# A selective scan on one core: the forcing term built from token-major blocks scaled by B and transposed, in place of products with diagonals of B

## The chip, the core and the metric

The kernel runs on one core of a Trainium2 chip. Its time is the time on the device, in microseconds, from one launch to the end; several runs are taken, and their median is the figure. Of one execution there is also a profile: for each engine (TensorE for matrix products, VectorE, ScalarE, GpSimd, SyncE for DMA), what it ran and what it waited for. The kernel before takes 28995.0 us, the median of three runs from 28984.81 to 29002.8.

## What is computed

The input `x` is an image of 256 x 256 positions with 128 channels. Two layers are applied, each to a group-normalised `x` and each added to `x`. Layer 0 is attention within rows, with a gate. Layer 1, where the change lies, is a two-dimensional selective scan. Cut to what matters:

```python
# layer 1; d = 256 channels, N = 16 states, L = 256 * 256 positions, K = 4 directions
xin, z = split(x @ in_proj_w.T)                  # 256 channels each
xc  = silu(conv3x3_depthwise(xin) + conv_b)
xs  = [xc by rows, xc by columns, rows reversed, columns reversed]
dts, B, C = split(xs @ x_proj_w)                 # 8, 16 and 16 numbers a position, for each k
dt  = softplus(dts @ dt_proj_w + dt_proj_b)
for l in range(L):                               # for each k, channel, state n
    h = h * exp(dt[l] * A[n]) + (dt[l] * xs[l]) * B[l, n]
    y[l] += h * C[l, n]                          # summed over n
y = sum over the four directions of (y + Ds * xs), brought back to one order
out = (layernorm(y) * silu(z)) @ out_proj_w.T
```

So for each direction, each of 256 channels and each of 16 states a recurrence runs over 65536 positions. Its forcing term is `(dt * x) * B[n]`: a factor of channel and position by a factor of state and position.

## The kernel before

**Tiling.** Layer 0 takes about the first 3.3 ms. Layer 1 then passes over the image four times, for the directions k = 0, 2, 1, 3 in this order. A pass has 64 chunks of 4 rows or columns, T = 1024 positions ("tokens"). Channels lie on the 128 partitions, in two blocks (j = 0, 1), and tokens along the free axis. A chunk has 32 units, each one channel block j and one state n: eight units (m = 0 to 7) for each of (g, j) = (0, 0), (0, 1), (1, 1), (1, 0), with n = 8g + m. There are 256 x 32 = 8192 units. Unit numbers below are places in a chunk, 0 to 31.

**A unit** needs a decay `exp(dt * A)` (`decay`, L854, ScalarE), a feed (the forcing term), a scan over 1024 tokens on VectorE (`scan`, L936), the scan's last column copied as the next chunk's start (`carry`, L950, ScalarE), a product of the states by C (`times_c`, L944) and a sum over n of the products (`add_up`, L910: eight 128 x 128 transposes on TensorE, which accumulate in PSUM into a tile with tokens on the partitions). Four kinds of unit share the work out (`KINDS`, by m: "AACBACCB" for k = 0, "AABBAABE" for the others; E is a B where (g, j) = (1, 1)):

- A: the decay goes to PSUM; GpSimd makes the feed, `xu * b`, with B of this state broadcast to all partitions by a DMA (`feed`, L861, `load_b`); GpSimd makes the product by C.
- C: as A, but VectorE makes the product by C.
- B: the decay goes to SBUF; TensorE makes the feed, in PSUM (`feed_turned`, L874); VectorE makes the product by C.
- E: TensorE makes the feed, GpSimd the product by C.

So 16 of the 32 units in a chunk of the last three passes have a feed by TensorE (m = 2, 3, 6, 7 in each of four groups), and 8 of 32 in the first pass (m = 3, 7).

**TensorE's feed** works from a transposed copy of `u = dt * x`, `dtuT`, with tokens on the partitions: [token, block of 128 tokens t, channel]. For each t, a matrix product has the 128 tokens x 128 channels of `dtuT` on one side and, on the other, a diagonal matrix that holds B[:, n] of these 128 tokens: it transposes the block back to [channel, token] and multiplies by B at once. `diagonal` (L867) makes such a diagonal on ScalarE, as the identity times one column of B per token. Eight diagonals make a set for one state n; both channel blocks use it, and there are seven sets (`dgs`). TensorE runs an fp32 product as two hardware instructions, so the eight products of a unit are 16 in the profile.

**Rings.** Two PSUM slots "s" hold a decay (A, C) or a feed (B, E); four SBUF buffers "w" hold the feeds, decays or states; four "hc" hold products by C; three "b" and eight "c" the broadcast rows.

**Order.** The order is written out by hand (`manual_schedule`): each engine runs its instructions in the order in which the program issues them. `step(u)` (L1015) is called for each unit u and issues, in this order, the copy of the last scan's end, the decay of u + 1 (or of B and E units up to three ahead), GpSimd's feed of u + 3, transposes of finished products, TensorE's feed of u + 1, side work, diagonals, then the scan of u and its product by C.

Diagonals come from a queue: `plan` (L956) enters eight for each state with a first and a due unit, and `run_diagonals` (L1007) issues up to `RATE` of them a step, none in a step in which a ScalarE piece of side work was issued, unless due. The first unit allowed is that in which the set seven sets older is used last.

Side work (`prep`, `finish`, `adds`, `normalise`) is cut into pieces by generators, and `run_sides` (L981) issues up to `PIECES` TensorE pieces in a step, by u % 4. `prep` of the chunk after next or the next computes the convolution (first pass), the projections to B, C and dt (L581 to L605), the softplus of dt on ScalarE, `u = dt * x` on GpSimd (`xu`, L616), and the transposes of B and of u (`dtp` in its names) to `bT` and `dtuT`. `adds` adds the residual term by products with a diagonal of D (`dD`, L793) and the sums of earlier passes, in PSUM, to y. The transposes of u wait for unit 22 of the chunk before, or later:

```python
yield from through(at1 + 3 + j if k == 0 else max(22, at1 + 4 + j), [
```

Of the kernel before, what the change touches and what calls it, by code (L numbers as in the profile page):

```python
# [15 lines left out]
P = 128  # L16
# [297 lines left out]
def _layer1(tc, ctx, const, dram, ident, vec, mr, a, x1, x1T, out):  # L314
# [88 lines left out]
    hcs = Ring(p1, "hc", 4, [P, T])  # L403
    brs = Ring(p1, "b", 3, [P, T])
    crs = Ring(p1, "c", GS, [P, T])
    dgs = Ring(p1, "dg", 7, [P, TB, P])
    dtuTs = Ring(p1, "dtuT", 2, [P, TB, D])
    bTs = Ring(p1, "bT", 2, [P, TB, ST])

# [59 lines left out]
    def prep(i):  # L469
# [165 lines left out]
        yield from through(0, [(f"btp_{i}", [turn_b], leave_b)])  # L635
        w["dtuT"] = dtuTs.take(f"dtuT_{i}")
        for j in range(ND):
            yield from through(at1 + 3 + j if k == 0 else max(22, at1 + 4 + j), [
                turned(
                    w["dtuT"][:, 4 * q : 4 * q + 4, j * P : (j + 1) * P],  # L640
                    lambda u, q=q: xu[j][:, (4 * q + u) * P : (4 * q + u + 1) * P],
                    f"dtp_{i}_{j}_{q}",
                )
                for q in range(QT)
            ], "e")
            w["ready"] = j + 1
# [185 lines left out]
        kind = KINDS[work[u // SU][0]][u % GS]  # L832
        return ("B" if kind == "E" and u % SU // GS == 2 else kind) in kinds

    in_psum, in_sbuf, states, prod, bt, ct, diag = {}, {}, {}, {}, {}, {}, {}
    fed = [u for u in range(total) if is_kind(u, "AC")]

    def load_b(r):
# [21 lines left out]
        in_sbuf[u] = ops.take(f"w_{u}")  # L860
        nc.gpsimd.tensor_tensor(in_sbuf[u], live[i]["xu"][j], bt.pop(u), ALU.mult)  # L861

    def diagonal(i, n, t):

        if t == 0:
            diag[i, n] = dgs.take(f"dg_{i}_{n}")
        nc.scalar.mul(diag[i, n][:, t, :], ident, live[i]["bT"][:, t, n : n + 1])  # L867

    def feed_turned(u):
        i, p, g, j, n, m = at(u)  # L870
        assert live[i]["ready"] > j and not any(t[2:4] == (i, n) for t in queue)
        in_psum[u] = slots.take(f"s_{u}")
        for t in range(TB):
            nc.tensor.matmul(  # L874
                in_psum[u][:, t * P : (t + 1) * P], live[i]["dtuT"][:, t, j * P : (j + 1) * P],
                diag[i, n][:, t, :], start=True, stop=True,
            )

    def load_sum(i, j):

# [70 lines left out]


    queue = []
    uses = []

    def plan(i):  # L956


        for g in range(2):
            for m in range(GS):  # L960
                u = SU * i + 2 * GS * g + m
                if is_kind(u, "BE"):
                    uses.append(u + GS)
                    s = uses[-1 - dgs.n] - 1 if len(uses) > dgs.n else -SU
                    for t in range(TB):
                        queue.append((s, u - 2, i, g * GS + m, t))

    RATE = {0: (1, 2, 2, 1), 1: (2, 3, 3, 2), 2: (2, 3, 3, 2), 3: (2, 3, 3, 2)}
    PIECES = {0: (2, 2, 2, 3), 1: (1, 1, 1, 2), 2: (1, 1, 1, 2), 3: (1, 1, 1, 2)}
    sides = []  # L970

    class Side:
# [31 lines left out]
                sides.remove(d)  # L1004
        return taken

    def run_diagonals(u, most):  # L1007
        while queue and queue[0][0] <= u and (most > 0 or queue[0][1] <= u):
            if live[queue[0][2]].get("bT") is None:
                assert queue[0][1] > u  # L1010
                return
            diagonal(*queue.pop(0)[2:])
            most -= 1

    def step(u):  # L1015
# [38 lines left out]
        if q == 3 and is_kind(u + 3, "BE"):  # L1054
            decay(u + 3)
        if ok(u):
            run_diagonals(u, 0 if taken else RATE[work[i][0]][q])
            scan(u)
            times_c(u)
        while after:  # L1060
# [23 lines left out]
    with tc.manual_schedule():  # L1084
        whole(prep(0))
        plan(0)
        for r in range(brs.n):
            load_b(r)
        for m in range(GS):
            load_c(0, m)  # L1090
        sides.append(Side(prep(1), 0))
        for u in range(-14, -4):
            run_sides(u)
        run_diagonals(0, 2 * TB)
        for u in range(-4, total + 2 * SU):
            step(u)
            if u >= total + 4 and not sides:
                break
        assert not (sides or queue or late or after or prod or states)
# [83 lines left out]
```

## Time and profile before

The profiled execution has a span of 28988.8 us. Its rows, for the whole span:

| what | busy us | share | instructions |
|---|---|---|---|
| VectorE | 26363.1 | 91% | 17323 |
| TensorE products | 25085.4 | 87% | 169780 |
| GpSimd | 24175.9 | 83% | 10253 |
| ScalarE | 20821.1 | 72% | 41137 |
| TensorE weight loads | 19655.6 | 68% | 169780 |
| span of the profiled execution | 28988.8 | | |
| median of three runs | 28995.0 | | |

The mean clock granted to TensorE is 0.945 of full speed. The rows that the change touches, as groups of instructions, with the mean of one: feeds on TensorE 57344 of 291 ns, transposes of products 65536 of 280 ns, diagonals on ScalarE 14336 of 392 ns, GpSimd's products by C 4416 of 2363 ns and its feeds 4608 of 2364 ns, scans on VectorE 2335 to 2347 ns.

How to read this: a busy time on TensorE is not work at its peak, since its products are pipelined and their ends modelled. In a group's row, the last part is idle time of the engine just before these instructions and the instruction that ended most of it. A wait for several instructions is put down to the one that came last.

### The profile page before, as it was taken

Reading aid. Unit: us, or ns where it says so; the run is one execution under the profiler, and the core shown is the slowest. Engines: PE = TensorE matmul, PEld = TensorE weight load, DVE = VectorE, ACT = ScalarE, POOL = GpSimd, SP = SyncE. Lnnn points to the kernel's source line nnn. Section 1 sums busy time; section 2 is a strip of 40 time slices with the busy share of each in tenths; the row PEclk is TensorE's granted clock in tenths of the full one; section 3 lists DMA queues with packets and bytes.
Section 4 is the critical chain, followed back from the end, with each engine's and each line's share of the span. In section 5 each row is a group of like instructions: output and inputs, shape, how many; then the busy total and the mean of one; then the engine's idle time right before and its main releaser. Section 6 shows DMA issues by size and latency. Waiting matters only on the chain. (4 is left out here: it accounts for less than half of the span.)

```text
span 28988.8 us, 455370 instructions
## 1 busy us (share of the span) xinstructions
PE 25085.4 (87%) x169780; PEld 19655.6 (68%) x169780; DVE 26363.1 (91%) x17323; ACT 20821.1 (72%) x41137; POOL 24175.9 (83%) x10253
## 2 busy tenths in 40 slices
PE   8888888899988888888888888888888888888888
PEld 5555566666666677777777677777777667667666
DVE  7888799999999999999999999999999888888888
ACT  4555566666666777777777777777777777777777
POOL 3444588888888899999999999999999888888888
PEclk8888899999999999999999999999999999999999
DMA  3111366666666666666666666666666555555555
GB/s 97 56 55 55 120 232 231 232 233 233 233 233 232 235 232 234 233 230 235 231 236 233 222 228 225 223 226 224 224 228 204 187 186 190 183 187 188 183 189 170
DMA packets 2487616, 5803.35 MB, mean 200 GB/s; under 512 B 189921, under 2 KB 1248152, under 8 KB 2485400
## 3 DMA queue, kind: packets, MB, share of 16 engines
q1 hardware_dynamic: 2475896, 5739.62, 58.8%
q0 software_dynamic: 9504, 34.61, 0.4%
q8 instruction: 1339, 21.94, 0.3%
q14 instruction: 877, 7.18, 0.1%
HBM read 5236.61 MB, written 536.87 MB: 199 GB/s over the span
## 5 line engine op out<-in xcount | busy, mean ns | idle before, releaser
L944 POOL TENSOR_TENSOR hc<-w,c 128x1024 f32<-128x1024 f32 x4416 | 10413.3, 2363 | 2079.1 <-DVE w L936 1320.7
L861 POOL TENSOR_TENSOR w<-xu,b 128x1024 f32<-128x1024 f32 x4608 | 10863.0, 2364 | 442.1 <-DMA b<-bc 78.7
L910 PE MATMUL y<-ident,hc 128*128 128x128 f32 x65536 | 8668.4, 280 | 1520.6 <-POOL hc L944 867.7
L910 PEld LDWEIGHTS y<-ident,hc 128*128 128x128 f32 x65536 | 7528.2, 144 | 3126.6 <-issue 1135.0
L936 DVE TENSOR_TENSOR_SCAN w<-s,hst,w 128x1024 f32<-128x1024 f32 x3840 | 8868.8, 2335 | 585.2 <-ACT s L854 331.4
L874 PE MATMUL s<-dg,dtuT 128*128 128x128 f32 x57344 | 7674.3, 291 | 1860.1 <-DVE w L936 1250.8
L874 PEld LDWEIGHTS s<-dg,dtuT 128*128 128x128 f32 x57344 | 7174.9, 203 | 2982.7 <-DVE w L936 1099.1
L936 DVE TENSOR_TENSOR_SCAN s<-w,hst,s 128x1024 f32<-128x1024 f32 x3008 | 7059.2, 2347 | 1263.2 <-PE s L874 1218.8
L854 ACT ACTIVATE s<-dt,negA 128x1024 f32<-128x1024 f32 x4608 | 5149.6, 1118 | 107.7 <-ACT hst L950 0.2
L867 ACT ACTIVATE dg<-ident,bT 128x128 f32<-128x128 f32 x14336 | 4827.9, 392 | 6.6 <-PE s L874 0.4
L944 DVE TENSOR_TENSOR hc<-s,c 128x1024 f32<-128x1024 f32 x3776 | 4622.9, 1224 | 203.1 <-DMA c<-bc 4.0
L854 ACT ACTIVATE w<-dt,negA 128x1024 f32<-128x1024 f32 x3584 | 4095.0, 1143 | 155.8 <-POOL hc L944 155.2
L950 ACT COPY hst<-s 128x1 f32<-128x1 f32 x3776 | 586.6, 155 | 4293.0 <-DVE hc L944 4097.1
L186 POOL TENSOR_TENSOR bias<-tri,mk 128x2048 f32<-128x2048 f32 x256 | 1164.0, 4547 | 1462.3 <-DVE ss L204 1303.7
L525 PE MATMUL cv<-xn,wtap 128*128 128x512 f32 x4608 | 2134.5, 595 | 10.3 <-ACT xn L514 10.3
L936 DVE TENSOR_TENSOR_SCAN s<-s,hst,w 128x1024 f32<-128x1024 f32 x768 | 1795.4, 2338 | 0.5 <-ACT s L854 0.4
L950 ACT COPY hst<-w 128x1 f32<-128x1 f32 x4416 | 808.4, 183 | 844.6 <-DVE w L936 805.7
L210 ACT ACTIVATE ss<-ss,nm 128x256 f32<-128x256 f32 x2048 | 866.5, 497 | 740.4 <-DVE nm L208 739.5
L936 DVE TENSOR_TENSOR_SCAN w<-w,hst,s 128x1024 f32<-128x1024 f32 x576 | 1346.0, 2337 | 2.6 <-PE s L874 2.1
L525 PEld LDWEIGHTS cv<-xn,wtap 128*128 128x128 f32 x4608 | 805.5, 190 | 702.6 <-issue 687.9
L616 POOL TENSOR_TENSOR xu<-dt,xu 128x1024 f32<-128x1024 f32 x512 | 1199.8, 2360 | 78.5 <-DMA b<-bc 78.5
L602 PE MATMUL dp<-xd,dtw 8*128 8x512 f32 x2048 | 1116.3, 640 | 0.3 <-ACT dt L605 0.3
(171 smaller groups left out, 22400.8 us busy)
## 6 DMA issues: line engine op xcount, KB each, us to landing
b<-bc SPq DMA_DIRECT2D x4608, 512.0 KB, 4.1
c<-bc SPq DMA_DIRECT2D x4096, 512.0 KB, 6.7
xc_d<-xu SPq DMA_DIRECT2D x256, 512.0 KB, 5.2
yrow_d<-ys SPq DMA_DIRECT2D x128, 1024.0 KB
xu<-xc_d SPq DMA_DIRECT2D x256, 512.0 KB, 6.2
yl<-yrow_d SPq DMA_DIRECT2D x512, 256.0 KB, 6.9
xcT_d<-xs SPq DMA_DIRECT2D x128, 512.0 KB, 2.9
xl<-xc_d SPq DMA_DIRECT2D x128, 512.0 KB, 7.1
```

The costliest lines, as they stand in the source:

```text
L186: nc.gpsimd.tensor_tensor(bias, tri.rearrange("p b h k -> p (b h) k"), st["mk"][:, r : r + 1, :].to_broadcast([P, NB * H, N]), ALU.add,)
L525: nc.tensor.matmul(pc, wtap[:, j, t, :], xn[:, 2 * q + u : 2 * q + u + 2, v : v + N], start=t == 0, stop=t == 8,)
L602: [lambda pt, j=j, q=q: nc.tensor.matmul(pt, dtw[:, k, j, :], xd[0:R, q * 512 : (q + 1) * 512], start=True, stop=True)],
L616: nc.gpsimd.tensor_tensor(xu[j], dt[j], xu[j], ALU.mult)
L854: nc.scalar.activation(dA, live[i]["dt"][j], AF.Exp, scale=negA[:, work[i][0] * ND + j, n : n + 1])
L861: nc.gpsimd.tensor_tensor(in_sbuf[u], live[i]["xu"][j], bt.pop(u), ALU.mult)
L867: nc.scalar.mul(diag[i, n][:, t, :], ident, live[i]["bT"][:, t, n : n + 1])
L874: nc.tensor.matmul(in_psum[u][:, t * P : (t + 1) * P], live[i]["dtuT"][:, t, j * P : (j + 1) * P], diag[i, n][:, t, :], start=True, stop=True,
L910: nc.tensor.matmul(w["y"][:, t, :], hc[:, t * P : (t + 1) * P], ident, is_transpose=True, start=first and t % 4 == 0, stop=last and t % 4 ...
L936: nc.vector.tensor_tensor_scan(rev(states[u]), rev(a), rev(b), hst[k][:, j, n : n + 1], ALU.mult, ALU.add)
L944: eng.tensor_tensor(prod[u], states[u], ct[i, n], ALU.mult)
L950: nc.scalar.copy(hst[k][:, j, n : n + 1], states.pop(u)[:, end : end + 1])
```

## The change

The feed of B and E units still works from `dtuT` and ends in PSUM with channels on the partitions, but its two steps are divided differently. For each state n and block t, `scale_b` multiplies the 128 tokens x 256 channels of `dtuT` by B[:, n], one number per partition (token), and writes both channel blocks, each to its slot of `bxs`. ScalarE does this for seven of the eight blocks t, GpSimd for t = 3. TensorE then transposes the scaled blocks of 128 x 128 by the identity, eight for a unit, with one hardware instruction each.

`bxs` has seven slots of [128, 8, 128], as many bytes as the seven sets of diagonals; a state takes two slots, one for each channel block, and each is free again after its feed. The queue's first unit becomes u - 14, its due unit stays u - 2, and a scaling waits until both channel blocks of `dtuT` are there (`ready`) and two slots are free. The transposes of u to `dtuT` may now be issued from `at1 + 4` for both blocks, rather than from unit 22. `PIECES` gives side work two TensorE pieces in every step of the last three passes (one in three steps of four and two in the fourth before), and three in the first two of each four steps of the first pass (two before).

```diff
--- before.py
+++ after.py
@@ -403,7 +403,9 @@
     hcs = Ring(p1, "hc", 4, [P, T])
     brs = Ring(p1, "b", 3, [P, T])
     crs = Ring(p1, "c", GS, [P, T])
-    dgs = Ring(p1, "dg", 7, [P, TB, P])
+    NBX = 7
+    bxs = p1.tile([P, NBX, TB, P], F32, tag="bx", name="bxs")
+    bx_free = list(range(NBX))
     dtuTs = Ring(p1, "dtuT", 2, [P, TB, D])
     bTs = Ring(p1, "bT", 2, [P, TB, ST])
 
@@ -635,7 +637,7 @@
         yield from through(0, [(f"btp_{i}", [turn_b], leave_b)])
         w["dtuT"] = dtuTs.take(f"dtuT_{i}")
         for j in range(ND):
-            yield from through(at1 + 3 + j if k == 0 else max(22, at1 + 4 + j), [
+            yield from through(at1 + 3 + j if k == 0 else at1 + 4, [
                 turned(
                     w["dtuT"][:, 4 * q : 4 * q + 4, j * P : (j + 1) * P],
                     lambda u, q=q: xu[j][:, (4 * q + u) * P : (4 * q + u + 1) * P],
@@ -832,7 +834,7 @@
         kind = KINDS[work[u // SU][0]][u % GS]
         return ("B" if kind == "E" and u % SU // GS == 2 else kind) in kinds
 
-    in_psum, in_sbuf, states, prod, bt, ct, diag = {}, {}, {}, {}, {}, {}, {}
+    in_psum, in_sbuf, states, prod, bt, ct, scaled = {}, {}, {}, {}, {}, {}, {}
     fed = [u for u in range(total) if is_kind(u, "AC")]
 
     def load_b(r):
@@ -860,21 +862,27 @@
         in_sbuf[u] = ops.take(f"w_{u}")
         nc.gpsimd.tensor_tensor(in_sbuf[u], live[i]["xu"][j], bt.pop(u), ALU.mult)
 
-    def diagonal(i, n, t):
+    def scale_b(i, n, t):
 
         if t == 0:
-            diag[i, n] = dgs.take(f"dg_{i}_{n}")
-        nc.scalar.mul(diag[i, n][:, t, :], ident, live[i]["bT"][:, t, n : n + 1])
+            scaled[i, n, 0], scaled[i, n, 1] = sorted((bx_free.pop(0), bx_free.pop(0)))
+        s0, s1 = scaled[i, n, 0], scaled[i, n, 1]
+        dst = bxs[:, s0 : s1 + 1 : s1 - s0, t, :]
+        src = live[i]["dtuT"][:, t, :].rearrange("p (j d) -> p j d", j=ND)
+        b = live[i]["bT"][:, t, n : n + 1]
+        if t == 3:
+            nc.gpsimd.tensor_scalar(dst, src, b, 1.0, ALU.mult, ALU.mult)
+        else:
+            nc.scalar.mul(dst, src, b)
 
     def feed_turned(u):
         i, p, g, j, n, m = at(u)
-        assert live[i]["ready"] > j and not any(t[2:4] == (i, n) for t in queue)
+        assert not any(t[2:4] == (i, n) for t in queue)
         in_psum[u] = slots.take(f"s_{u}")
+        slot = scaled.pop((i, n, j))
         for t in range(TB):
-            nc.tensor.matmul(
-                in_psum[u][:, t * P : (t + 1) * P], live[i]["dtuT"][:, t, j * P : (j + 1) * P],
-                diag[i, n][:, t, :], start=True, stop=True,
-            )
+            nc.tensor.transpose(in_psum[u][:, t * P : (t + 1) * P], bxs[:, slot, t, :], ident)
+        bx_free.append(slot)
 
     def load_sum(i, j):
 
@@ -951,7 +959,6 @@
 
 
     queue = []
-    uses = []
 
     def plan(i):
 
@@ -960,13 +967,11 @@
             for m in range(GS):
                 u = SU * i + 2 * GS * g + m
                 if is_kind(u, "BE"):
-                    uses.append(u + GS)
-                    s = uses[-1 - dgs.n] - 1 if len(uses) > dgs.n else -SU
                     for t in range(TB):
-                        queue.append((s, u - 2, i, g * GS + m, t))
+                        queue.append((u - 14, u - 2, i, g * GS + m, t))
 
     RATE = {0: (1, 2, 2, 1), 1: (2, 3, 3, 2), 2: (2, 3, 3, 2), 3: (2, 3, 3, 2)}
-    PIECES = {0: (2, 2, 2, 3), 1: (1, 1, 1, 2), 2: (1, 1, 1, 2), 3: (1, 1, 1, 2)}
+    PIECES = {0: (3, 3, 2, 3), 1: (2, 2, 2, 2), 2: (2, 2, 2, 2), 3: (2, 2, 2, 2)}
     sides = []
 
     class Side:
@@ -1004,12 +1009,13 @@
                 sides.remove(d)
         return taken
 
-    def run_diagonals(u, most):
+    def run_scales(u, most):
         while queue and queue[0][0] <= u and (most > 0 or queue[0][1] <= u):
-            if live[queue[0][2]].get("bT") is None:
-                assert queue[0][1] > u
+            s, due, i, n, t = queue[0]
+            if live[i].get("bT") is None or live[i]["ready"] < ND or (t == 0 and len(bx_free) < 2):
+                assert due > u, (u, due, live[i]["ready"], bx_free)
                 return
-            diagonal(*queue.pop(0)[2:])
+            scale_b(*queue.pop(0)[2:])
             most -= 1
 
     def step(u):
@@ -1054,7 +1060,7 @@
         if q == 3 and is_kind(u + 3, "BE"):
             decay(u + 3)
         if ok(u):
-            run_diagonals(u, 0 if taken else RATE[work[i][0]][q])
+            run_scales(u, 0 if taken else RATE[work[i][0]][q])
             scan(u)
             times_c(u)
         while after:
@@ -1091,7 +1097,7 @@
         sides.append(Side(prep(1), 0))
         for u in range(-14, -4):
             run_sides(u)
-        run_diagonals(0, 2 * TB)
+        run_scales(0, 2 * TB)
         for u in range(-4, total + 2 * SU):
             step(u)
             if u >= total + 4 and not sides:
```

## The prediction

> **What bounds the kernel now.** I read the page's rows of busy time first, then the windows view with one window for each of the four passes of layer 1 (directions 0, 2, 1, 3; their borders are the first and last scans in the timeline), because the page's averages mix layer 0 with four passes whose limits differ.
>
> ```profile
> core 0: us, PE busy (x) PEld busy (x) DVE busy (x) ACT busy (x) POOL busy (x), PEclk, DMA share, GB/s
> 3342.00:9903.00 6561.00, 5857.97 (x31900) 4159.94 (x31899) 6212.63 (x3328) 4442.65 (x7864) 5717.02 (x2494) 0.93 0.68 232
> 9903.00:16014.00 6111.00, 5354.79 (x39162) 4448.75 (x39161) 5681.48 (x2881) 4638.23 (x9595) 5551.53 (x2367) 0.98 0.69 233
> 16014.00:22054.00 6040.00, 5178.77 (x37115) 4279.13 (x37113) 5679.93 (x2882) 4667.29 (x9616) 5548.99 (x2369) 0.97 0.66 225
> 22054.00:28947.00 6893.00, 5835.07 (x40089) 4815.70 (x40088) 6047.28 (x4077) 5366.21 (x10622) 5961.24 (x2617) 0.93 0.56 187
> ```
>
> Divided by 64 chunks: the second pass takes 95.5 us a chunk, of which VectorE works 88.8 and GpSimd 86.7; the third 94.4, 88.7, 86.7; the first 102.5, 97.1, 89.3; the fourth 107.7, 94.5, 93.1, with ScalarE at 83.8. So VectorE is the bound, GpSimd 2 us behind it in the middle passes, and all that any change of feeding can win is VectorE's idle time, 5.4 to 13.2 us a chunk. What ends that idle time, by pass (waits view of VectorE, second pass, then fourth):
>
> ```profile
> DVE s L936 <- PE s L874: 333.7, 206, 4.6
> DVE w L936 <- POOL w L861: 34.5, 50, 0.7
> ...
> DVE s L936 <- PE s L874: 385.9, 227, 3.3
> DVE w L936 <- ACT s L854: 314.7, 265, 2.2
> ```
>
> The scans wait for TensorE's feeding products (L874): 5.2 us a chunk in the second pass. In the fourth ScalarE's decays (L854) cost another 4.9. The timeline shows how such a wait of 2.02 us arises, at unit 14 of a chunk (places 0 to 31 below):
>
> ```profile
> 13469.51 2.36 POOL L944 TENSOR_TENSOR hc<-w,c 128x1024 f32<-128x1024 f32 x1
> ...
> 13471.92 1.09 PE L910 MATMUL y<-ident,hc 128*128 128x128 f32 x8 [0.41 <-POOL hc L944]
> ...
> 13476.93 1.95 PE L874 MATMUL s<-dg,dtuT 128*128 128x128 f32 x16
> ...
> 13478.92 2.35 DVE L936 TENSOR_TENSOR_SCAN s<-w,hst,s 128x1024 f32<-128x1024 f32 x1 [2.02 <-PE s L874]
> ```
>
> The GpSimd row is unit 9's product by C, ending at 13471.87; TensorE stands in order behind it, then has 5.0 us of other work before the feed and 1.95 in it. GpSimd has worked without a pause since unit 4, so the feed is late because GpSimd is.
>
> **What the Trainium skill says.** "TensorE: Matmul & The Clock Gate", Part 4: a transpose is a product in transpose mode, which doesn't count as TensorE activity for its clock in the same way. The trace agrees on the form, not clearly on the clock: an fp32 product of L874 takes two instructions (57344 for 28672), a transpose of L910 one. "ScalarE: Activation LUTs", What ACT_TABLE_LOAD costs: 0.833 ns an element. "GPSIMD Engine Reference", 4.1 Engine selection: one-input work is near line rate, two-input work isn't; 3.1: 512 elements took 769 ns in a good one-input loop.
>
> **The change, part by part.** The prices:
>
> ```profile
> L944 POOL TENSOR_TENSOR hc<-w,c 128x1024 f32<-128x1024 f32 x4416 | 10413.3, 2363 | 2079.1 <-DVE w L936 1320.7
> L910 PE MATMUL y<-ident,hc 128*128 128x128 f32 x65536 | 8668.4, 280 | 1520.6 <-POOL hc L944 867.7
> L874 PE MATMUL s<-dg,dtuT 128*128 128x128 f32 x57344 | 7674.3, 291 | 1860.1 <-DVE w L936 1250.8
> L867 ACT ACTIVATE dg<-ident,bT 128x128 f32<-128x128 f32 x14336 | 4827.9, 392 | 6.6 <-PE s L874 0.4
> L660 POOL TENSOR_SCALAR rstd<-mv 128x8 f32<-128x8 f32 x64 | 15.3, 239 | 324.0 <-DVE mv L658 324.0
> L509 POOL COPY xn<-xn 128x516 f32<-128x516 f32 x63 | 38.2, 607 | 0.0
> ```
>
> *TensorE.* A feed of 16 instructions (1.95 us in the timeline) becomes 8 transposes (1.04 us, as eight of L910): 0.9 us off each of 3584 feeds, 3260 us of TensorE's time. Only what lies before a late scan counts.
>
> *ScalarE.* Per chunk of the last three passes 64 scalings of 128 elements become 56 of 256. Back to back one costs 0.32 us (0.98 for three); 128 more elements add 0.107, an estimate with that skill page's 0.833 ns: 0.42. 56 x 0.42 - 64 x 0.32 = +3 us a chunk. Over most of the chunk ScalarE's wait to copy a finished scan's end hides it (L950 on L944, 4097 us in the page's rows); with that cover gone it would cost 3 x 64 = 192 us a pass.
>
> *GpSimd.* 8 new scalings of 256 elements a chunk (4 in the first pass). The trace has no such row. Below: 239 ns plus 248 elements at the copy's at most 607/516 = 1.18 ns gives 0.53, at 0.83 ns 0.45. Above: two-input rate, 0.77 (239 + 248 x 2.13, the slope between the 2048-element bias at 4547 and L944); a scalar read from memory might bring it to 1.0. I take 0.5 us, 0.56 with the hand-over. This loads the engine that is 2 us from the bound: 86.7 + 8 x 0.56 = 91.2 busy, and with the 0.08 us that the timeline shows before each feed product (37 operations, 2.385 from start to start, are 88.2) 92.7.
>
> *New waits.* Each transpose waits for its own scaling, so the fourth waits for GpSimd. Unit 7's sits behind hc4 and feed 8: hc4 starts at 14.4, so it ends at 19.8, the feed at 20.6; the scan wants it at 20.0: 0.7 us of stall that was not there. Behind it in TensorE's queue stand the products of units 4 and 6, whose buffers GpSimd reuses four units on: no one waits yet. The other scalings lie four units ahead. ScalarE's new waits, for slots that TensorE has just read, have the copy of a scan's end behind them and, behind that, a feed product on GpSimd; they end within the running scan, so I cost them at nothing, and at up to 1 us for each of four a chunk if TensorE is late.
>
> *Moves.* With more pieces a step, projections move ahead, their stores (SP's queue) by a unit or two with them, ahead of B and C loads that land in 4 to 7 us and are asked for three units or more ahead, so at no cost: before unit 14's feed now stand two projections and eight dD products, not one and four: the 5.0 us become 6.0, which eats the 0.9 gained. The two products u = dt x on GpSimd (L616, 2.36 each) move from behind feed 25 to behind feed 21 (second and third pass), into the 2.6 us that GpSimd has idle before hc20, and the softplus with its two table loads from unit 20 or 14 to 17 (second, third), 17 (first), 9 (fourth).
>
> **The sum, by walking one chunk** in the changed order, from hc4, where GpSimd waits for a scan (hc is a product by C). The steps are the timeline's starts: a unit takes VectorE 2.26 us when GpSimd multiplies, 3.55 with its own product (B, C), GpSimd 2.33 a product by C and 2.44 a feed. Second pass, times from the chunk's first scan: hc9 ends at 34.6 (was 33.4; two scalings lie before it), 6.0 and 1.04 later unit 14 scans, at 41.7 (was 40.5); xu ahead of hc20 ends feed 25 at 74.5, 1.5 us after its scan could start; unit 30's old stall of 2.6 us shrinks to 0.6, because hc25 ends at 81.6 and no longer stands behind the two u products. Stalls 0.7 + 0.3 + 2.2 + 1.5 + 0.6 + 0.3 = 5.6 against 6.0: the chunk takes about 94.8, -0.7 x 64 = -45 us. Third pass: same order, less to win (its unit-30 stall was 1.4): 94.7 against 94.4, +20. Fourth: the feed of unit 6 no longer waits for scalings (-1.4), the softplus block moved to unit 9 delays unit 12 by 2 us but frees units 14 and 16 (-1.0, -1.8), unit 30 keeps its stall: about -2.9 a chunk, -186. First: the Silu block stands before unit 12, where it costs 1.0, not before unit 15's feed, where it cost 2.9; softplus costs 1.0 at unit 20 for 0.8 at 23 and 24: -1.5, -96. Layer 0 and the first 90.6 us wait for the convolution are untouched. Sum -307; the median stands 6 us above the profiled span (28995.0, 28988.8), so 28690. GpSimd idles less in this walk than I can be sure of, and TensorE, less busy, will be granted a lower clock: +0.4 us on each of two chains in the middle passes, +50. I say 28740, its own range 28550 to 28900.
>
> **Rivals.** (a) *GpSimd becomes the bound (slower).* Place: the middle passes. Each 0.1 us of the scaling adds 0.55 us a chunk there and little elsewhere: about +80 us per 0.1. The gain is gone at 0.8 us; at 1.1 the time is 29250. For: 86.7 of 94 us. Against: the rows above. (b) *TensorE's clock falls.* In the first 160 us, where only transposes run, the granted clock is 0.80. At 0.8 the 7 us before units 14 and 30 take 8.6: +3 us a chunk in three passes, 29250. Against: 75% busy rather than 60%, projections remain. (c) *All waits on feeds vanish.* The page's row of scans has 1219 us of them. GpSimd's floor of 92.7 then sets the middle passes, -2.8 and -1.7 a chunk, the others lose their 6.0 and 3.3 of these waits less 0.3: (2.8 + 1.7 + 5.7 + 3.0) x 64 = 840, 28150. For: that is the largest wait; against: the timeline's GpSimd chain. (d) *It moves nothing*: gains in the fourth pass are met by losses in the third, 28990.
>
> **How the numbers follow.** The forecast 0.44, (a) 0.24, (b) 0.1, (c) 0.1, (d) 0.12. Faster than 28937 (0.2% is 58 us, about what this kernel's measurement can tell): all of (c), all but 0.03 of the forecast: 0.51. Slower: (a), (b) and 0.02 of (d): 0.36. The rest, 0.13, is within. Range: 28400 to 29300, leaving out (c) but for its nearer fifth (0.08), the far third of (b) and a fifth of (a) (0.08).
>
> **What would show it.** In the changed profile: GpSimd's scaling at 0.45 to 0.6 us, over 93% busy in the middle passes; feeds of 8 at 1.04 us; VectorE's waits for feeds down by a third only, at units 7, 14; more "w" waits on GpSimd's feeds near unit 25; the fourth pass near 6700 us, the middle ones within 60 of before. Wrong if the scaling takes over 0.8 us, if the clock in the second pass is under 0.9, or if ScalarE's decays hold the fourth pass longer than now.

## The result, and the profile after

The changed kernel takes 29100.8 us, the median of five runs from 29092.48 to 29108.21, against 28995.0 (28984.81 to 29002.8, five runs): a ratio of 1.0037, with a 95% interval from 1.0024 to 1.0050. It is slower by 106 us. The forecast was 28740, faster by 255; the measured time lies inside its range, on the other side of no change.

The windows of the changed kernel, one for each pass (length; busy time and instructions of the TensorE products, weight loads, VectorE, ScalarE and GpSimd; granted clock, DMA share, GB/s):

```profile
3343.00:9993.00 6650.00, 5577.53 (x27798) 3796.44 (x27796) 6218.46 (x3328) 4521.85 (x7600) 5835.46 (x2749) 0.90 0.68 228
9993.00:16111.00 6118.00, 4805.20 (x30971) 3820.99 (x30972) 5676.63 (x2881) 4842.72 (x9091) 5782.65 (x2879) 0.91 0.69 233
16111.00:22227.00 6116.00, 4757.96 (x28914) 3735.27 (x28913) 5675.99 (x2881) 4840.69 (x9095) 5781.67 (x2882) 0.88 0.67 222
22227.00:29060.00 6833.00, 5205.66 (x31901) 4013.60 (x31900) 6029.80 (x4078) 5598.37 (x10120) 6200.31 (x3127) 0.87 0.57 188
```

VectorE's work is what it was. TensorE has 420 to 630 us less in each of the last three passes, at a lower clock; GpSimd has 231 to 239 us more in each, ScalarE 173 to 232. Measured from the first scan of a pass to the first of the next and divided by 64, in us a chunk:

| pass | before | forecast | after |
|---|---|---|---|
| first (k = 0) | 102.5 | 101.0 | 103.9 |
| second (k = 2) | 95.5 | 94.8 | 95.6 |
| third (k = 1) | 94.4 | 94.7 | 95.6 |
| fourth (k = 3) | 107.7 | 104.8 | 106.8 |

So the forecast was 2.9, 0.8, 0.9 and 2.0 us a chunk too low. The scans of the kernel before, then the scans of the changed kernel and the groups of instructions that the change made (out, in, count; busy, mean ns; idle time before them and what ended it):

```profile
L936 DVE TENSOR_TENSOR_SCAN w<-s,hst,w 128x1024 f32<-128x1024 f32 x3840 | 8868.8, 2335 | 585.2 <-ACT s L854 331.4 <-POOL w L861 108.1 <-PE cv L525 90.6
L936 DVE TENSOR_TENSOR_SCAN s<-w,hst,s 128x1024 f32<-128x1024 f32 x3008 | 7059.2, 2347 | 1263.2 <-PE s L874 1218.8 <-ACT hst L950 17.8 <-ACT s L854 13.7
```

```profile
L944 DVE TENSOR_TENSOR_SCAN w<-s,hst,w 128x1024 f32<-128x1024 f32 x3840 | 8890.4, 2337 | 1294.5 <-ACT s L856 999.3 <-POOL hc L952 144.7 <-ACT hst L958 77.2
L944 DVE TENSOR_TENSOR_SCAN s<-w,hst,s 128x1024 f32<-128x1024 f32 x3008 | 7040.2, 2340 | 493.8 <-PE s L884 492.7
L876 ACT ACTIVATE bxs<-dtuT,bT 128x256 f32<-128x256 f32 x12544 | 5607.8, 499 | 278.5 <-PE s L884 277.5
L884 PE MATMUL s<-ident,bxs 128*128 128x128 f32 x28672 | 4475.0, 305 | 2594.8 <-DVE w L944 1728.8 <-ACT hst L958 527.1 <-POOL bxs L874 314.9
L874 POOL TENSOR_SCALAR bxs<-dtuT,bT 128x256 f32<-128x256 f32 x1792 | 859.1, 479 | 7.3 <-ACT dtuT L485 1.3
```

The change did what it was meant to: the scans that read a feed in PSUM waited 1219 us for TensorE before and 493 now (E units, not shown, 2 and 100). But the scans whose decay is in PSUM (the first row) wait 999 us for a decay of ScalarE, where it was 331. Of the 999, 93.5 are the single wait before the first scan of layer 1, which the profile before puts down to a convolution product (90.6); 906 against 331 is the fair comparison. The wait went from one engine to another.

### The profile page after: what moved, and what is told of

Its sections match the earlier page's. It is cut to its first block, busy times and chain, and to the rows that moved or that the text cites. A ratio compares the mean times of both kernels' runs of the same rounds, so it can differ in the third digit from the quotient of the medians.

```text
span 29102.7 us, 397457 instructions
## 1 busy us (share of the span) xinstructions
PE 23210.6 (80%) x141108; PEld 17322.5 (60%) x141108; DVE 26345.1 (91%) x17323; ACT 21511.9 (74%) x39345; POOL 24998.0 (86%) x12045
## 5 line engine op out<-in xcount | busy, mean ns | idle before, releaser
L918 PE MATMUL y<-ident,hc 128*128 128x128 f32 x65536 | 9613.8, 302 | 2689.0 <-POOL hc L952 880.6
L918 PEld LDWEIGHTS y<-ident,hc 128*128 128x128 f32 x65536 | 8390.1, 156 | 4374.0 <-POOL hc L952 1523.9
L884 PE MATMUL s<-ident,bxs 128*128 128x128 f32 x28672 | 4475.0, 305 | 2594.8 <-DVE w L944 1728.8
L876 ACT ACTIVATE bxs<-dtuT,bT 128x256 f32<-128x256 f32 x12544 | 5607.8, 499 | 278.5 <-PE s L884 277.5
L884 PEld LDWEIGHTS s<-ident,bxs 128*128 128x128 f32 x28672 | 3659.6, 157 | 3607.1 <-DVE w L944 1281.3
L856 ACT ACTIVATE s<-dt,negA 128x1024 f32<-128x1024 f32 x4608 | 5148.9, 1117 | 107.7 <-ACT hst L958 0.5
```

The costliest lines, as they stand in the source:

```text
L856: nc.scalar.activation(dA, live[i]["dt"][j], AF.Exp, scale=negA[:, work[i][0] * ND + j, n : n + 1])
L876: nc.scalar.mul(dst, src, b)
L884: nc.tensor.transpose(in_psum[u][:, t * P : (t + 1) * P], bxs[:, slot, t, :], ident)
L918: nc.tensor.matmul(w["y"][:, t, :], hc[:, t * P : (t + 1) * P], ident, is_transpose=True, start=first and t % 4 == 0, stop=last and t % 4 ...
```

## Where the new waits are

Idle time of VectorE before the scan of each unit, as a mean over the chunks, shows the places. In the second and third pass the wait at unit 30 (2.5 and 1.6) is gone, and one at unit 13 is there (2.8 and 2.3), which was nothing before. The timeline of the changed kernel at such a unit 13 of the second pass (start, duration, engine and line, then in brackets what the engine had waited for):

```profile
11930.73 0.47 POOL L874 TENSOR_SCALAR bxs<-dtuT,bT 128x256 f32<-128x256 f32 x1
11931.17 4.70 POOL L952 TENSOR_TENSOR hc<-w,c 128x1024 f32<-128x1024 f32 x2
...
11933.57 1.15 ACT L856 ACTIVATE w<-dt,negA 128x1024 f32<-128x1024 f32 x1 [1.77 <-POOL hc L952]
...
11936.38 1.00 ACT L929 COPY part<-y 128x1024 f32<-128x1024 f32 x1
...
11937.53 1.82 PE L918 MATMUL y<-ident,hc 128*128 128x128 f32 x8 [1.97 <-ACT part L929]
...
11939.28 2.79 PE L583 MATMUL xp<-xu,xpw 128*40 128x512 f32 x4
...
11942.11 0.58 ACT L591 COPY xd<-xp 40x512 f32<-40x512 f32 x1 [2.72 <-PE xp L583]
...
11944.61 1.12 ACT L856 ACTIVATE s<-dt,negA 128x1024 f32<-128x1024 f32 x1
...
11945.83 2.35 DVE L944 TENSOR_TENSOR_SCAN w<-s,hst,w 128x1024 f32<-128x1024 f32 x1 [2.83 <-POOL hc L952]
```

Read it downwards as one chain. GpSimd's scaling pushes back its product by C, which frees a "w" buffer; ScalarE's decay waits 1.77 us for that buffer; the copy of y to `part`, behind it in ScalarE's queue, is late; TensorE, which may not overwrite y before, stands 1.97 us; the projection behind it is late; ScalarE's copy of the projection waits 2.72 us for it; and behind that copy stand the decays, the last of them unit 13's own. The scan's record names a product of GpSimd, but the scan doesn't read it: what it reads is the decay of 11944.61, which ended at 11945.73, 0.1 us before the scan.

ScalarE's wait for the projection is not larger than before (172.4 us in the second pass, 178.7 before). What changed is its place: in the kernel before nearly all of it falls in the time of unit 14, in the changed one in that of unit 12, ahead of unit 13's decay. In the third pass the end of the chain is the same (169.6 us of waits for the projection), but it begins on TensorE: the transposes for unit 7 wait 2.48 us for GpSimd's scaling (at 18042.59), and what stands behind them is late.

In the first pass the new waits are at units 27 and 29 (1.25 and 1.45). At unit 27 four products of the convolution (1.88 us) now stand ahead of the feed on TensorE. The timeline of the changed kernel at unit 29:

```profile
6553.93 0.58 ACT L536 COPY xu<-cv 128x512 f32<-128x512 f32 x1 [5.83 <-POOL w L863]
...
6554.61 1.12 ACT L856 ACTIVATE s<-dt,negA 128x1024 f32<-128x1024 f32 x1
...
6555.82 2.36 DVE L944 TENSOR_TENSOR_SCAN s<-s,hst,w 128x1024 f32<-128x1024 f32 x1 [2.00 <-ACT s L856]
```

With more pieces a step the convolution is done earlier, and its first result is to be copied to `xu`. That is a ring of two buffers, and the older one is still read by GpSimd's feeds. ScalarE stands for 5.83 us, and the decay and the scan behind it. Over the pass it stood so 61 times, 320.9 us.

In the fourth pass the wait at unit 12 grew from 0.8 to 3.9, and at unit 9 from 1.3 to 2.4. ScalarE's timeline there, in the changed kernel:

```profile
24393.91 1.28 ACT L613 ACT_TABLE_LOAD   x1
24395.20 2.19 ACT L613 ACTIVATE dt<-dt,vecs 128x1024 f32<-128x1024 f32 x2
...
24397.96 1.08 ACT L670 ACTIVATE ys<-ys,mrs,rstd 128x256 f32<-128x256 f32 x2
...
24399.02 1.00 ACT L929 COPY part<-y 128x1024 f32<-128x1024 f32 x1
...
24400.92 1.30 ACT L876 ACTIVATE bxs<-dtuT,bT 128x256 f32<-128x256 f32 x3
...
24402.28 1.28 ACT L856 ACT_TABLE_LOAD   x1
24403.57 1.12 ACT L856 ACTIVATE s<-dt,negA 128x1024 f32<-128x1024 f32 x1
```

From 24393.91 to 24403.57, 9.7 us, ScalarE does no decay: the softplus and its two table loads have moved into the stretch in which it also normalises y, copies `part` and scales. In the kernel before, the softplus starts in unit 14, after that stretch. The scan of unit 9 comes before it (at 24391.37), so this explains unit 12 alone; what makes unit 9 later was not isolated.

## The experiments

Three theories of the loss. "Moves": the side work that the change brings forward (PIECES, the earlier transposes of u) stands ahead of decays in ScalarE's queue. "GpSimd": its eight scalings a chunk cost the middle passes their gain. "Clock": transposes let TensorE's granted clock fall (0.945 to 0.888 over the span), and all its work grows. None of the kernels below leaves out any part of the computation. Each ratio is taken to runs of the kernel before made together with that kernel, whose medians lie between 28972 and 28996, so it can differ a little from the quotient of the times shown. What each pass took, in us a chunk:

| kernel | us | ratio to before, 95% interval | first | second | third | fourth |
|---|---|---|---|---|---|---|
| before | 28995.0 | | 102.5 | 95.5 | 94.4 | 107.7 |
| change | 29100.8 | 1.0037 [1.0024, 1.0050] | 103.9 | 95.6 | 95.6 | 106.8 |
| e1: moves alone | 29213.7 | 1.0079 [1.0064, 1.0094] | 104.4 | 95.5 | 94.5 | 109.0 |
| e3: change, products with the identity | 29508.5 | 1.0182 [1.0166, 1.0197] | 105.4 | 96.6 | 96.2 | 110.1 |
| e4: change, all scalings on ScalarE | 28821.8 | 0.9945 [0.9930, 0.9959] | 103.9 | 93.2 | 93.0 | 107.3 |
| e5: change, fewer pieces | 29090.0 | 1.0036 [1.0023, 1.0048] | 102.8 | 96.6 | 96.8 | 105.6 |
| e6: e4, old pieces in first and fourth | 28643.1 | 0.9881 [0.9866, 0.9896] | 104.5 | 93.3 | 93.0 | 103.9 |
| e7: e6, GpSimd scales in the fourth | 28745.6 | 0.9917 [0.9902, 0.9932] | 104.6 | 93.3 | 93.0 | 105.5 |
| e8: change, two scalings of eight on GpSimd | 29769.6 | 1.0270 [1.0253, 1.0287] | 104.1 | 99.6 | 99.5 | 109.0 |
| e9: e4, GpSimd scales to a spare buffer | 29131.4 | 1.0050 [1.0035, 1.0065] | 104.0 | 95.6 | 95.6 | 107.3 |
| e10: e6, GpSimd scales in the first | 28535.4 | 0.9848 [0.9831, 0.9864] | 102.9 | 93.2 | 92.9 | 104.0 |
| e11: e10 with three edits | 29118.2 | 1.0050 [1.0035, 1.0065] | 107.3 | 96.8 | 92.4 | 105.5 |
| e12: e10, other pieces in the middle | 28450.3 | 0.9813 [0.9796, 0.9829] | 102.7 | 92.8 | 92.3 | 103.9 |

**e1, the moves without the feed.**

```diff
 # the kernel before
-            yield from through(at1 + 3 + j if k == 0 else max(22, at1 + 4 + j), [
+            yield from through(at1 + 3 + j if k == 0 else at1 + 4, [
-    PIECES = {0: (2, 2, 2, 3), 1: (1, 1, 1, 2), 2: (1, 1, 1, 2), 3: (1, 1, 1, 2)}
+    PIECES = {0: (3, 3, 2, 3), 1: (2, 2, 2, 2), 2: (2, 2, 2, 2), 3: (2, 2, 2, 2)}
```

> The kernel before with the diagonals kept, and only the side work moved as in the change: the new PIECES and the earlier transposes of u. Theory 'moves' (the loss is made by side work that stands ahead of decays in ScalarE's queue): unit 13 of the second and third pass waits 1.5 us or more a chunk for its decay, as in the changed kernel (2.8 and 2.3), the softplus block stalls units 9 and 12 of the fourth pass by 4 us or more together, and the time is 29150 or more, since the wins of the cheaper feed are absent. Theory 'clock' (the loss is made by transposes, with which TensorE is granted 0.89 in place of 0.945): the clock stays at 0.94 or more, unit 13 waits under 0.8 us, and the time is 28950 to 29050.

Measured: slower by 0.79%, as "moves" said, with the clock at 0.944. But the loss is in the first (+1.9) and the fourth pass (+1.2) alone: units 9 and 12 of the fourth wait 4.4 us together, 3.6 of them at unit 12 (unit 9 waits less than before), and units 27 and 29 of the first 3.3. The middle passes lose 0.1 at most, and unit 13 waits 0.2 and 0.3; that part of "moves" is refuted. The moves cost 121 + 79 us by themselves; on top of them the new feed, with GpSimd's scalings, wins about 113 (29213.7 to 29100.8).

**e3, the transposes as products.**

```diff
 # the change
-            nc.tensor.transpose(in_psum[u][:, t * P : (t + 1) * P], bxs[:, slot, t, :], ident)
+            nc.tensor.matmul(
+                in_psum[u][:, t * P : (t + 1) * P], bxs[:, slot, t, :], ident, start=True, stop=True
+            )
```

> The changed kernel, with each transpose of a scaled block replaced by an ordinary product with the identity (two hardware instructions rather than one). Scalings, moves and order are those of the change. Theory 'clock': the granted clock comes back to 0.93 or more, the wait at unit 13 falls under 1 us, and in spite of feeds of 1.95 us the time is 28950 to 29080, at or below that of the change. Theory 'moves': unit 13 still waits over 2 us, the waits for feeds grow by 2 to 3 us a chunk because each feed is 0.9 us longer, and the time is 29200 to 29500.

Measured: the clock comes back, 0.937 over the span. The second pass in the windows of this kernel, where the changed one had 0.91:

```profile
10093.00:16277.00 6184.00, 5398.97 (x39171) 4583.84 (x39170) 5696.51 (x2881) 4859.88 (x9091) 5788.29 (x2879) 0.97 0.68 230
```

Data and order are those of the change, so the form of that one instruction decides the clock. This agrees with what the Trainium skill states in "TensorE: Matmul & The Clock Gate", Part 4: a transpose doesn't count as TensorE activity in the same way. A rival is that TensorE is merely less busy (79% of the second pass in the change, 87% here). Busy share alone doesn't fit all passes: the first of e6, below, is 87% busy at 0.88, the third of the kernel before 86% busy at 0.97. But the work of these passes differs, so the two aren't fully separated.

Unit 13's wait shrinks to 0.3 and 0.4. That isn't shown to be the clock's doing, since VectorE now waits longer at other units (1.3 and 1.5 at unit 7, 2.2 and 2.1 at unit 14), which gives GpSimd time. The whole is 408 us above the change: the transposes are worth more than the clock that they cost, and a return to products doesn't mend the loss. The lower clock does have a price on TensorE: the 65536 transposes of finished products, the same in both kernels, take 302 ns each in the change and 284 here (280 before). How much of that reaches the kernel's time isn't separated by any run here.

**e4, all scalings on ScalarE.**

```diff
 # the change
-        if t == 3:
+        if t == TB:                # never: all eight on ScalarE
```

> The changed kernel with the eighth scaling on ScalarE too, none on GpSimd. Theory 'GpSimd' (eight scalings of 0.48 us on the engine that is nearest to the bound cost the middle passes their gain): GpSimd's busy share in them falls by 3.8 us a chunk, the stalls at units 3, 7 and 25 (1.3 to 1.9 us a chunk together) go, and the middle passes take 94.0 us a chunk or less; whole time 28950 or less. Theory 'moves': units 3, 7 and 25 gain at most 1 us, ScalarE has 3.5 us more work a chunk, the waits for decays grow in the fourth pass, and the time is 29050 to 29250.

Measured: 28821.8, faster than before by 0.55%. The middle passes fall by 2.4 and 2.6 us a chunk, 154 + 165 us; the first stays, the fourth rises by 0.5. Second pass in this kernel's windows:

```profile
9998.00:15962.00 5964.00, 4808.00 (x30970) 3776.65 (x30971) 5678.35 (x2881) 5026.18 (x9604) 5556.42 (x2367) 0.93 0.71 239
```

and ScalarE's waits in it, in the kernel before, in the changed kernel and in this one:

```profile
ACT w L854 <- POOL hc L944: 34.0, 49, 1.4
ACT xd L589 <- PE xp L581: 178.7, 127, 2.6
```

```profile
ACT w L856 <- POOL hc L952: 216.8, 126, 1.9
ACT xd L591 <- PE xp L583: 172.4, 65, 2.7
```

```profile
ACT w L856 <- POOL hc L952: 77.0, 99, 1.1
ACT xd L591 <- PE xp L583: 75.0, 78, 2.4
```

GpSimd does 226 us less, and both links of the chain shorten: the decays wait about a third as long for GpSimd's products, the projection's copy less than half as long. Unit 13 waits 0.9 in place of 2.8. ScalarE did 183 us more and was not missed. "GpSimd" expected 94.0 or less in these passes and gets it; that units 3, 7 and 25 lose their waits holds too (1.3 us in the second pass, 1.8 in the third), but as much again comes from unit 13, which it didn't name (1.9 and 1.5).

**e5, fewer pieces.**

```diff
 # the change
-    PIECES = {0: (3, 3, 2, 3), 1: (2, 2, 2, 2), 2: (2, 2, 2, 2), 3: (2, 2, 2, 2)}
+    PIECES = {0: (2, 2, 2, 3), 1: (2, 1, 2, 1), 2: (2, 1, 2, 1), 3: (1, 1, 1, 2)}
```

> The changed kernel with the PIECES of before in the first and fourth pass, and (2, 1, 2, 1) in the second and third (those of before can't be had there, since the transposes of u would not be ready for the first scaling). Theory 'moves': the fourth pass loses the stall of 3.9 us at unit 12 or most of it and falls to 105 us a chunk or less, the first falls under 103, unit 13 of the middle passes waits under 1.5 us; time 28650 to 28900. Theory 'clock' or 'GpSimd': each pass within 0.7 us a chunk of the changed kernel, time 28950 to 29150, stalls of the same size elsewhere.

Measured: the time lies outside what "moves" expected; the passes tell why. The first falls by 1.15 and the fourth by 1.2 us a chunk (to 105.6, a little above the 105 expected), as e1 says they should: ScalarE's waits for the ring `xu` behind GpSimd's feeds no longer appear among its larger waits in the first pass, unit 12 of the fourth waits 1.3 in place of 3.9. The middle passes lose 1.0 and 1.2. Unit 13 there does fall to about 1 us, but units 1 to 3 wait 2.4 and 2.5 together, where it was 0.5 and 0.6.

**e8 and e9, GpSimd's time or a wait for it.** In the change the fourth transpose of each unit waits for GpSimd. e8 adds a second such scaling:

```diff
 # the change
-        if t == 3:
+        if t in (3, 7):
```

> The changed kernel with two scalings of eight on GpSimd (t = 3 and 7) in place of one. Theory 'GpSimd's time' (each scaling of 0.48 us there costs the middle passes 0.3 us of their end, as the step from none to one did with 2.4 and 2.6 us a chunk): the second and third pass take 97.5 to 99 us a chunk, whole time 29350 to 29600. Theory 'one wait too many' (what costs is that a transpose waits for two engines rather than one, and the second scaling adds no such wait): 95 to 96.3 us a chunk, time 29000 to 29200.

Measured: 99.6 and 99.5, 4.0 us a chunk more in both middle passes, where the first step cost 2.5; passes and total lie above what "GpSimd's time" gave. But this run doesn't decide between the two theories. What TensorE waits for in the second pass of this kernel:

```profile
PE s L884 <- POOL bxs L874: 480.7, 192, 4.2
```

In the change this is 157.4 us. At unit 23 the eighth transpose stands 3.97 us (at 12073.40) for GpSimd's second scaling, which has a product and a feed ahead of it in GpSimd's queue. The scans of units 3 and 23 wait 2.7 and 2.9 us for such feeds; in the change they wait 0.5 and nothing. So the second scaling does add waits, against what the second theory assumed, and GpSimd isn't the bound: it is busy 94% of the pass, as in the change.

e9 leaves all scalings that are used on ScalarE, and lets GpSimd do its own for nobody:

```diff
 # the change
-        if t == 3:
-            nc.gpsimd.tensor_scalar(dst, src, b, 1.0, ALU.mult, ALU.mult)
-        else:
-            nc.scalar.mul(dst, src, b)
+        if t == 3 and work[i][0] != 3:
+            spare = p1.tile([P, T], F32, tag="yn", name=f"spare_{i}_{n}")
+            spare = spare[:, 0 : ND * P].rearrange("p (j d) -> p j d", j=ND)
+            nc.gpsimd.tensor_scalar(spare, src, b, 1.0, ALU.mult, ALU.mult)
+        nc.scalar.mul(dst, src, b)
```

> The kernel with all scalings on ScalarE (e4), and in the first three passes GpSimd also does the scaling that it did in the change, at the same place in its queue, but into a spare buffer that nobody reads. Theory 'GpSimd's time': the middle passes go back to 95 to 96.3 us a chunk, though no transpose waits for GpSimd. Theory 'the wait' (transposes that stand behind GpSimd's scaling): they stay at 93 to 93.6.

Measured: the middle passes take 95.55 and 95.56, those of the change 95.59 and 95.56. Second pass, windows of this kernel:

```profile
10000.00:16115.00 6115.00, 4873.67 (x30968) 3821.37 (x30968) 5682.07 (x2881) 5025.97 (x9603) 5786.06 (x2878) 0.91 0.69 233
```

No transpose waits for GpSimd here, and unit 13 waits 2.9 us, in the change 2.8. This settles the middle passes of the change: GpSimd's time alone, 230 us a pass, brings the whole loss back by way of the products and feeds behind it, and no wait of the transposes is needed. With two scalings of eight (e8) such waits come on top.

**e6, e7 and e10, the parts put together.**

```diff
 # e6: the change, with
-        if t == 3:
+        if t == TB:                # e7: t == 3 and work[i][0] == 3; e10: t == 3 and work[i][0] == 0
-    PIECES = {0: (3, 3, 2, 3), 1: (2, 2, 2, 2), 2: (2, 2, 2, 2), 3: (2, 2, 2, 2)}
+    PIECES = {0: (2, 2, 2, 3), 1: (2, 2, 2, 2), 2: (2, 2, 2, 2), 3: (1, 1, 1, 2)}
```

> All scalings on ScalarE, the PIECES of before in the first and fourth pass, those of the change in the middle passes. If the two losses found so far (GpSimd's scalings in the middle passes, side work that is moved too far ahead in the first and fourth) add up, the passes take 102.8, 93.2, 93.0 and 105.5 to 106.3 us a chunk and the whole 28640 to 28720. If they don't (ScalarE, with 8 more scalings a chunk, becomes late where side work is less early), the fourth pass takes 107 or more and the whole 28750 or more.

> As the run beside it (e6), but with the eighth scaling on GpSimd in the fourth pass alone, where GpSimd has 12 us a chunk to spare and ScalarE is the later one. If ScalarE is the later one there, the fourth pass is 0.3 to 1.0 us a chunk faster than in e6 (105.5), 20 to 60 us in all; if each GpSimd scaling costs wherever it stands, it is slower than in e6 by 1 us a chunk or more.

> As e6, but with the eighth scaling on GpSimd in the first pass alone, where e5 (which has it, with the same side work) took 102.8 us a chunk and e6 104.5. If the passes add up: first pass 102.8, the others as in e6, 28500 to 28560 in all. If the first pass of e5 was fast for another reason, it stays at 104 to 104.6 and the time at 28620 to 28660.

Measured: the middle passes of e6 are as expected, and so is the total, but that by two misses that cancel: the first pass takes 104.5, not 102.8, and the fourth 103.9, below the range given. In the fourth pass, then, GpSimd's eight scalings cost 1.6 us a chunk (e7), although GpSimd is idle 10% of it in e6; ScalarE was not the one that was late. In the first pass it is the other way: with these PIECES GpSimd's four scalings win 1.6 us (e10: 102.9), since without them unit 6 waits 2.5 us for its decay; with the PIECES of the change they win nothing (103.9 in the change and in e4). In e6 ScalarE waits 410 us in that pass for the convolution's products, in e10 301; why the same convolution is later there stays open. e10 takes 28535.4, as expected.

**e11 and e12.** e11 reads three edits by pass:

```diff
 # e10, with
-            nc.tensor.transpose(in_psum[u][:, t * P : (t + 1) * P], bxs[:, slot, t, :], ident)
+            nc.tensor.matmul(
+                in_psum[u][:, t * P : (t + 1) * P], bxs[:, slot, t, :], ident,
+                is_transpose=work[i][0] != 0, start=True, stop=True,
+            )
-    PIECES = {0: (2, 2, 2, 3), 1: (2, 2, 2, 2), 2: (2, 2, 2, 2), 3: (1, 1, 1, 2)}
+    PIECES = {0: (2, 2, 2, 3), 1: (1, 2, 2, 2), 2: (2, 2, 1, 2), 3: (1, 1, 2, 1)}
```

> As e10, with three more edits, one for each stretch, read by pass. First pass: feeds as products with the identity rather than transposes. If the lower clock that comes with transposes costs there (TensorE is 86% busy in it), the clock goes from 0.90 to 0.93 and the pass falls to 102.3 us a chunk or less; if the shorter feed is worth more than the clock, it rises to 103.5 or more. Middle passes: PIECES (2, 2, 1, 2) in the second and (1, 2, 2, 2) in the third; if the projections ahead of unit 13's decay cause the 0.9 and 1.4 us at units 13 and 14, one of them falls by 0.5 us a chunk or more, else both stay within 0.3 of 93.2 and 93.0 or rise. Fourth pass: PIECES (1, 1, 2, 1), in which 103.9 moves by no more than 0.7 if only how early the softplus is matters.

Measured: products in the first pass bring its clock from 0.90 to 0.92 and cost 4.4 us a chunk, so there too the shorter feed is worth far more than the clock. One TensorE piece less in the third of four steps costs the second pass 3.6; one less in the first of four wins the third pass 0.5, with unit 14's wait down from 1.3 to 0.5. The fourth pass loses 1.6, more than the 0.7 allowed. The edit keeps the number of pieces in four steps, but the softplus moves from unit 14 to unit 11 (its table load is at 24453.94), and unit 12 waits 4.4 us again, 1.7 in e10: the stall of the change comes back with the softplus, which bears out its cause. e12 takes the one gain:

```diff
 # e10, with
-    PIECES = {0: (2, 2, 2, 3), 1: (2, 2, 2, 2), 2: (2, 2, 2, 2), 3: (1, 1, 1, 2)}
+    PIECES = {0: (2, 2, 2, 3), 1: (1, 2, 2, 2), 2: (1, 2, 2, 2), 3: (1, 1, 1, 2)}
```

> As e10, with PIECES (1, 2, 2, 2) in both middle passes, which in e11's third pass took 92.4 us a chunk rather than 92.9. If the two passes are alike in this (their orders of work are the same on GpSimd and ScalarE), both take 92.3 to 92.7 and the time is 28450 to 28500; if the second differs (its projections and stores are others), its pass stays at 93.1 or rises and the time is 28500 or more.

Measured: 28450.3 us, with 92.8 (a little above what was expected) and 92.3 in the middle passes. Against the kernel before it is 1.9% faster, against the change 2.2%. Its second pass:

```profile
9918.00:15854.00 5936.00, 4753.52 (x30973) 3716.80 (x30972) 5681.40 (x2881) 5025.90 (x9602) 5555.19 (x2367) 0.94 0.72 240
```

VectorE is busy 96% of the middle passes (5681 of 5936 and 5682 of 5907), where it was 93 and 94% before. In the fourth, VectorE still stands idle for 630 us.

## Why the prediction was wrong, by its steps

**The prices** were right. Eight transposes take 1.04 to 1.07 us. Two scalings on ScalarE take 0.90 and three 1.31, so 0.40 to 0.41 for one more, with 0.42 forecast. A scaling on GpSimd takes 0.479 us, with 0.5 forecast. The Trainium skill states in "GPSIMD Engine Reference", 4.1 Engine selection, that work with one input is roughly at line rate there and work with two inputs is not. The change's own row agrees: above the 239 ns of the 128x8 row, 248 more elements took 240 ns, an estimate of 0.97 ns each, where the two-input rows give 2.13.

**What GpSimd's scalings cost** was right as a number: 0.55 us a chunk for each 0.1 us, or 2.6 for 0.48; e4 measures 2.4 and 2.6. That is luck in part, because 1.9 and 1.5 of it come at unit 13, by a path that the walk doesn't have. What the rest of the change wins in the middle passes was too high. The walk has it, without these scalings, at 94.8 - 2.6 = 92.2 and 94.7 - 2.6 = 92.1; e4 has 93.2 and 93.0. So rival (a)'s price was near and its threshold wrong: by a straight line between e4 (0.55% faster, no scaling on GpSimd) and the change (0.37% slower, 0.48 us each), an estimate, the gain of the whole kernel is gone at about 0.3 us, not at 0.8.

**The step that failed** is the account of ScalarE's in-order queue: in "Moves", which prices what is brought forward on TensorE and GpSimd, for the loads and for the softplus, but not the copies on ScalarE, and in the walk, in which GpSimd's delay meets VectorE only in feeds and products. Both followed the queues of GpSimd, SP and TensorE, and hardly that of ScalarE. Every TensorE piece that is brought forward has a copy on ScalarE behind it, and behind that copy stand decays. In the first and fourth passes the moves alone cost time (e1); in the middle passes they cost 0.1 at most, and it is GpSimd's scalings that make ScalarE's copies and decays late (e4, e9). By pass:

- First pass, 2.9 us a chunk too low (185 us). The stalls at units 12 and 20 were forecast at 1.0 each and measured 1.3 and 1.2. Units 27 and 29, 2.7 together, were not seen: the convolution's products stand ahead of a feed, and its copy waits on ScalarE for a ring of two, whose older buffer GpSimd still reads. The prediction doesn't ask when the ring comes free.
- Middle passes, 0.8 and 0.9 too low (52 and 56 us). The sum of the stalls is not far off, 5.6 forecast and 6.3 measured in the second pass, but its terms are. Unit 7's stall was forecast at 0.7 and measured 0.5 and 1.0; unit 14's at 2.2 and measured 1.4 and 1.3; unit 25's at 1.5 and measured 0.3. Unit 13's 2.8 and 2.3 weren't in the sum: the projections were let in at a cost to TensorE alone. That GpSimd's delay reaches VectorE through ScalarE, in the second pass by a "w" buffer that is freed late, was not in the walk.
- Fourth pass, 2.0 too low (126 us). The mechanism was named, the softplus block that "delays unit 12 by 2 us": it is 3.1 us there, since the block meets normalising, `part` and the scalings in the same stretch. The 1.1 more at unit 9 is not of the block, which starts later; with the old pieces unit 9 still waits 2.3 us (e5), and 1.6 without GpSimd's scalings (e6), so the moves aren't its cause. Unit 6's 1.3 and unit 16's 1.8 were won as forecast, of unit 14's 1.0 only half.

The sentence under "New waits" that costs ScalarE's waits "at nothing" is about another wait, that of the scalings for free slots. It measured 278 us, 175 of them in unit 29 of the fourth pass; whether a scan is later for it isn't shown.

Together 420 us. The 50 allowed for GpSimd and the clock, and the 6 by which the median was to stand above the span (it stands 2 below), taken off, leave about the 361 between 28740 and 29101.

**The rivals.** (a) was right that GpSimd's time is what costs in the middle passes (e9), at 0.48 us where it asked for more than 0.8; but GpSimd isn't the bound there, busy 94 to 95%, and the delay arrives by way of ScalarE. (b): the clock fell, in the second pass from 0.98 to 0.91 and in the third from 0.97 to 0.88, so "wrong if the clock in the second pass is under 0.9" was not reached; going back to the higher clock makes the kernel slower (e3). (c) did not come about: 593 us of the scans' waits for feeds remain. (d) came nearest in time, 28990, and half of its account holds: the fourth pass gained 60 us and the third lost 76, but the first lost 89 as well. "Waits for feeds down by a third only" was too cautious, they fell by half (1221 to 593 with the E units); "or if ScalarE's decays hold the fourth pass longer than now" was the test that told: 549.5 us there, with 314.7 before.

## What to carry to other kernels

When work is brought forward in a schedule that is written out by hand, follow every instruction that comes with it on every in-order queue, the evacuating copies first: what they wait for (a product, a ring's older reader) holds all that stands behind them. An engine with a few us to spare in a period is not free, and if it frees buffers for a third engine its delay arrives by way of that one; a spare copy of the instruction, which nobody reads, measures this directly. A change with several parts is best read by stage: here a change that wins 90 to 150 us in each middle pass (e4, e10) was hidden by two choices that it didn't need: scalings on GpSimd in the last three passes, and side work brought forward in the first and fourth.

## What was not expected of the hardware

The change and e3 differ in the form of one instruction, and TensorE is granted 0.888 with transposes and 0.937 with products by the same identity. And still the lower clock with half of the feeds' instructions is better by 408 us, 1.4%. A copy of GpSimd's scaling that nobody reads cost as much as the scaling that is used (95.6 us a chunk in both, 93.2 and 93.0 without), on an engine that is idle 5 to 7% of the time.
